# One tile or two for the small squares of a causal attention by elementwise products

## The chip, the cores and the metric

The kernel runs on one core of a Trainium2 chip. The metric is the device time of one execution in microseconds (us); lower is better. The engines are TensorE (PE in the profile), VectorE (DVE), ScalarE (ACT) and GpSimd (POOL); SyncE (SP) issues DMA transfers. Each engine works off its own queue in order, and semaphores tie the queues together.

## The reference

A block of four layers with residual additions on x of shape (8, 512, 256), all in float32: attention "a", a feed-forward network, attention "b" (ordinary causal attention, 16 heads of 16), and the same feed-forward network again. Attention "a" is the unusual one. It attends within each token's own features: per token and head, the 64 numbers of q, k and v are 64 positions of one feature, and the scores are the outer product of q and k under a causal mask.

```python
Q = (x @ Wq + bq).reshape(b, s, H, C) * inv_sqrt_c          # H = 16, C = 64
K = (x @ Wk + bk).reshape(b, s, H, C)
V = (x @ Wv + bv).reshape(b, s, H, C)
scores = jnp.einsum('bshq,bshk->bshqk', Q, K)                # an outer product per token and head
scores = jnp.where(jnp.triu(ones((C, C)), 1), -inf, scores)
attn = jnp.einsum('bshqk,bshk->bshq', softmax(scores), V).reshape(b, s, HID)
return attn @ Wo + bo
```

```python
h = silu(lin(x, w1) * w1_s) * (lin(x, w2) * w2_s)            # 256 -> 1024
h = gelu(lin(h, h1) * h1_s)                                  # 1024 -> 1024, twice
h = gelu(lin(h, h2) * h2_s)
return lin(h, w3) * w3_s                                     # 1024 -> 256
```

## The kernel before

Two streams run through the kernel at once. The first is attention "a" of batch b + 1, the second everything that follows for batch b (feed-forward, attention "b", feed-forward). The first uses POOL and DVE most, the second PE and ACT.

Attention "a" goes by units: one unit is 128 tokens (on the 128 partitions) and 4 of the 16 heads. There are 16 units a batch (4 groups of heads times 4 blocks of tokens) and 128 in all; "unit 9" below is the tenth of its batch. The causal triangle of 64 by 64 is cut into squares below the diagonal: one of 32 by 32, two of 16 by 16, four of 8, eight of 4, sixteen of 2, thirty-two of 1, and the diagonal. The squares of a unit are worked in four portions, `n_u`:

- 0 and 2: the squares of size 32, two heads each; 1: those of size 16; 3: all the small ones, sizes 8, 4, 2 and 1.
- Portions 0 to 2 have tiles `w` of 4096 columns, of which four rotate. Portion 3 has a tile `ws` of 2 x 1920 columns, and there is only one such tile.

The steps of a unit, each a method of `AttentionA`:

- `project` (PE, lines 841 and 846) and `keep_qk` (ACT): q, k and v of the unit.
- `scores` (line 893): the products of q and k. POOL makes those of portions 0, 1 and 2, in two halves of 1024 columns each; DVE makes the four of portion 3, one for each size (1024, 512, 256 and 128 columns), and the diagonal (line 872).
- `exps` (ACT, line 916; the diagonal at line 907): the exponentials, one instruction for each portion.
- `weigh` (DVE, lines 925 and 928): the exponentials times v, into the second half of the tile.
- `halve` (line 935): POOL issues a DMA that adds one half of the tile onto the other. `fold` (POOL, line 943) halves once more, for portion 2.
- `sums32` (PE, line 956, sixteen transposes, portion 0), `keep_sums`, `turn_sums` (line 1027) and `add32` (DVE, line 1038) sum portion 0 through PE. `gather` (DVE, line 1135) sums portions 1 and 2 and the sizes 8 and 4 of portion 3 by reductions.
- `adds` (POOL, line 1151) adds the rows that `gather` made to the unit's accumulator `acc`.
- `small_squares` (POOL): for size 2 it adds the two columns (line 1061, called the pair step below), and then adds the rows of size 2 and of size 1, straight from `ws`, to `acc` (line 1151 again). When these and `gather` are done, `ws` is free for the next unit.
- `invert` (DVE, line 1157), `divide` (POOL, line 1163), `turn_group` (PE), `keep_att` (ACT), `project_out` (PE), `new_x` (ACT): the quotient, the output projection and the new x.

The order on the engines is fixed by a table. Time is counted in slots, twelve to a unit; each row of `G['order']` gives a step its slot, counted from the unit's start, so that steps of up to four units lie side by side. Within a slot the row's place in the table decides. `G['first']` is the table of the first batch; from the second batch on, `G['shifts']` moves a step of one unit by some slots, and `G['bends']` moves the due time of the second stream in one unit. After each slot, the second stream is advanced by steps of an estimated length until it has caught up:

```python
            a.slot(at)
            ...
            due = at + 1 - 12 * NT * NG - 33
            due += BENDS[(at - 12) // 12 % (NT * NG)] if 0 < due < 12 * NT * NG * (NB - 1) else 0
            while spent * 12 * NT * NG < total * due:
                spent += next(done)
```

Of the second stream the text meets these: the row statistics of a new x (`moments`, DVE, line 600, after ACT's copy of the row at line 1472), the products of a hidden layer (PE, line 1453), and attention "b" with its scores (PE, lines 1599 and 1603), exponentials (ACT, line 1606) and values (PE, line 1611).

Of the kernel before, what the change touches and what calls it, by code (L numbers as in the profile page):

```python
# [16 lines left out]
P = 128  # L17
# [29 lines left out]
 'order': [[15, 'turn_sums', 0], [34, 'project_out'], [8, 'scores', 2, 1, 2], [10, 'exps', 2],  # L47
           [22, 'small_squares'], [-120, 'load'], [-26, 'normalise'], [6, 'exps', 1], [13, 'sums32', 0],
           [23, 'adds', 3], [16, 'keep16'], [9, 'weigh', 1], [-1, 'scores', 0, 0, 2], [20, 'add16'],
           [32, 'turn_group'], [-22, 'turn_x'], [11, 'fold', 0], [12, 'turn16'], [6, 'halve', 0],  # L50
           [11, 'scores', 3, 0, 1], [22, 'keep_sums', 2], [-30, 'ahead'], [14, 'sums16'], [22, 'add32', 2],
           [12, 'weigh', 2], [18, 'turn_sums', 2], [-8, 'project'], [10, 'halve', 1], [36, 'new_x'],
           [25, 'divide'], [13, 'weigh', 3], [7, 'scores', 2, 0, 2], [4, 'scores', 1, 1, 2], [17, 'fold', 2],
           [32, 'keep_att'], [-5, 'keep_qk'], [12, 'exps', 3], [12, 'halve', 2], [13, 'keep_sums', 0],
           [18, 'add32', 0], [18, 'gather', 3], [24, 'invert'], [13, 'gather', 1], [16, 'adds', 1],
           [20, 'sums32', 2], [4, 'weigh', 0], [3, 'exps', 0], [1, 'scores', 1, 0, 2], [-22, 'keep_x'],
           [0, 'scores', 0, 1, 2]],
# [3 lines left out]
           'order': [[21, 'small_squares'], [23, 'adds', 3], [21, 'sums32', 2], [-23, 'turn_x'],  # L61
                     [0, 'scores', 0, 1, 2], [4, 'scores', 1, 0, 2], [16, 'keep16'], [15, 'turn16'],
                     [29, 'divide'], [26, 'invert'], [19, 'add32', 0], [6, 'scores', 2, 0, 2],
                     [6, 'halve', 0], [-1, 'scores', 0, 0, 2], [-27, 'normalise'], [9, 'fold', 0],
                     [7, 'exps', 1], [10, 'exps', 2], [20, 'gather', 3], [15, 'turn_sums', 0],
                     [4, 'weigh', 0], [23, 'turn_sums', 2], [15, 'weigh', 3], [-120, 'load'], [-30, 'ahead'],
                     [17, 'adds', 1], [15, 'gather', 1], [19, 'sums16'], [10, 'scores', 3, 0, 1],
                     [23, 'add32', 2], [8, 'weigh', 1], [10, 'halve', 1], [36, 'new_x'],
                     [4, 'scores', 1, 1, 2], [13, 'weigh', 2], [-5, 'keep_qk'], [-20, 'keep_x'],
                     [6, 'scores', 2, 1, 2], [14, 'exps', 3], [31, 'turn_group'], [21, 'add16'],  # L70
                     [14, 'sums32', 0], [21, 'keep_sums', 2], [32, 'keep_att'], [13, 'fold', 2],
                     [14, 'keep_sums', 0], [-8, 'project'], [34, 'project_out'], [13, 'halve', 2],
# [16 lines left out]
 'shifts': [[6, 'gather', 1, 1], [5, 'project', 1], [7, 'add32', 2, 1], [13, 'weigh', 3, 1],  # L89
            [15, 'exps', 2, -1], [5, 'keep_sums', 2, -1], [15, 'scores', 2, 1, 2, 1], [4, 'project_out', -1],  # L90
            [13, 'adds', 3, -1], [5, 'divide', 1], [1, 'scores', 1, 1, 2, -1], [4, 'weigh', 0, 1],
            [14, 'scores', 0, 1, 2, 2], [8, 'gather', 3, 2], [11, 'weigh', 1, 1], [14, 'weigh', 2, -1],
            [7, 'scores', 1, 1, 2, -1], [2, 'normalise', 1], [2, 'turn_sums', 2, -1], [7, 'fold', 2, 1],
            [15, 'project', -1], [3, 'turn_sums', 0, 1], [12, 'turn_sums', 0, -1], [5, 'exps', 0, -1],
            [0, 'keep_att', 1], [9, 'turn_sums', 2, -1], [12, 'scores', 2, 0, 2, -2], [15, 'sums32', 0, -2],
            [1, 'turn_sums', 2, -1], [8, 'halve', 0, 1], [12, 'turn_sums', 2, -1], [15, 'add32', 0, -1],
            [11, 'turn_sums', 2, -1], [1, 'exps', 2, -1], [10, 'turn_sums', 2, 1], [4, 'scores', 0, 1, 2, -1],
            [5, 'gather', 3, 2], [5, 'exps', 1, -1], [10, 'scores', 2, 1, 2, 1], [13, 'gather', 1, -1],
            [13, 'gather', 3, -1], [4, 'divide', 1], [6, 'exps', 0, -2]],
 'bends': [0, 0, 0, 0, 0, 0, 0, 0.5, 0.5, 0, 0, 0, 1, 0, 0, -2],  # L100
 'sp': []}
# [244 lines left out]
def fast_path(ctx: ExitStack, tc: tile.TileContext, k, t, flag):  # L346
# [292 lines left out]
    units = (((32, 0, 2),), ((16, 0, 4),), ((32, 2, 2),), ((8, 0, 4), (4, 0, 4), (2, 0, 4), (1, 0, 4)))  # L639
    NU = len(units)  # L640
    SMALL = 1920
# [37 lines left out]
    def pieces(w, n, off, nsq, cols, b, n_u, parts):  # L679
# [7 lines left out]
        if n == 8 and kind8(b) == "pe":  # L687
            e, ev = (
                w[:, a * SMALL + off : a * SMALL + off + nsq * n * n].rearrange("p (j x i) -> p j x i", j=n, i=n)
# [3 lines left out]
        elif n < 16:  # L693
            e, ev = (
                w[:, a * SMALL + off : a * SMALL + off + nsq * n * n].rearrange("p (x i j) -> p x i j", i=n, j=n)
# [41 lines left out]
    BENDS = G.get("bends", [0] * NT * NG)  # L737

    class AttentionA:
# [126 lines left out]
        def scores(self, b, i, g, n_u, part, parts):  # L866
# [7 lines left out]
            if part == 0:  # L874
                if n_u < NU - 1 and (n_u != 1 or G["rot"] == 4):
                    w = wt.tile([P, 4096], F32, tag="w", name=f"w_{b}_{i}_{g}_{n_u}", bufs=G["rot"])
                elif n_u == 1:
                    w = wt.tile([P, 4096], F32, tag="w16", name=f"w16_{b}_{i}_{g}")
                else:
                    w = wt.tile([P, 2 * SMALL], F32, tag="ws", name=f"ws_{b}_{i}_{g}")  # L880
                self.live[b, i, g, n_u] = w
                self.ps = []
                for n, off, nsq, cols in squares(units[n_u]):
                    self.ps += list(pieces(w, n, off, nsq, cols, b, n_u, 2))
                if not hasattr(self, "pieces"): self.pieces = {}
                self.pieces[b, i, g, n_u] = self.ps
            ps = self.pieces[b, i, g, n_u]
            on_pool = n_u in (0, 2) or (n_u == 1 and part < p16(b)) or (n_u == 3 and "P3" in on(b))
            eng, q = (nc.gpsimd, kt[:, 1]) if on_pool else (nc.vector, qv[:, 0])
            mine = ps if parts == 1 else [ps[part]]  # L890
            for e, ev, rows, columns in mine:
                shape = list(e.shape)
                eng.tensor_tensor(  # L893
                    e, rows(q).to_broadcast(shape), columns(kt[:, 0]).to_broadcast(shape), ALU.mult
                )
# [7 lines left out]
        def exps(self, b, i, g, n_u):  # L903
# [8 lines left out]
            elif n_u < NU - 1:  # L912
                e = w.rearrange("p (b a r) -> p a b r", a=2, b=units[n_u][0][0] // JB)[:, 0]
            else:
                e = w[:, :SMALL]
# [14 lines left out]
        def halve(self, b, i, g, n_u):  # L930

            assert (b, i, g, n_u, "w") in self.seen
# [4 lines left out]
        def fold(self, b, i, g, n_u):  # L937

            if kind(b, n_u) == "pe16": return
# [5 lines left out]
        def sums32(self, b, i, g, n_u):  # L945

            how = kind(b, n_u)
            assert (b, i, g, n_u, "h" if how == "pe16" else "f") in self.seen
# [4 lines left out]
            n = 16 if how == "pe16" else 8  # L953
# [75 lines left out]
        def add32(self, b, i, g, n_u):  # L1029

            if kind(b, n_u) == "dve":
                self.adds(b, i, g, n_u)
                return
# [18 lines left out]
        def small_squares(self, b, i, g):  # L1052

            assert (b, i, g, NU - 1, "w") in self.seen
            self.seen.add((b, i, g, NU - 1, "s"))
            w = self.live[b, i, g, NU - 1]
            for n, off, nsq, cols in squares(units[NU - 1]):
                if n <= 2 and n not in reds(b):
                    both = self.columns_of(w, n, off, nsq)
                    if n == 2:  # L1060
                        (nc.vector if "small" in on(b) else nc.gpsimd).tensor_tensor(both[..., :1], both[..., :1], both[..., 1:], ALU.add)
                    self.add_rows(b, i, g, n, cols, both[..., 0], "small")
            self.done_small(b, i, g)

        def done_small(self, b, i, g):

            if all((b, i, g, NU - 1, what) in self.seen for what in ("r", "s") + (("8",) if kind8(b) == "pe" else ())):
                self.live.pop((b, i, g, NU - 1))

        def sums8(self, b, i, g):  # L1070

            if kind8(b) == "dve": return
            assert (b, i, g, NU - 1, "w") in self.seen
            self.seen.add((b, i, g, NU - 1, "8"))
            w = self.live[b, i, g, NU - 1]
            h = G.get("half8", 1)
            self.take(h, 0, 1)
            for r in range(2):
                for j in range(8):
                    nc.tensor.matmul(  # L1080
                        bank_half(h)[:, r * P : (r + 1) * P], w[:, r * SMALL + j * P : r * SMALL + (j + 1) * P], ident,
# [31 lines left out]
        def gather(self, b, i, g, n_u):  # L1113

            if n_u == 1 and kind(b, 1) != "dve": return
            assert (b, i, g, n_u, "h" if n_u < NU - 1 else "w") in self.seen
            self.seen.add((b, i, g, n_u, "r"))
            w = self.live[b, i, g, n_u]
            if n_u < NU - 1: self.live.pop((b, i, g, n_u))
# [20 lines left out]
        def adds(self, b, i, g, n_u):  # L1140
            if (b, i, g, n_u) not in self.sums: return
            for args in self.sums.pop((b, i, g, n_u)):
                self.add_rows(*args, f"adds{n_u}")
# [75 lines left out]

    class Weights:  # L1220
# [4 lines left out]
        def __init__(self):  # L1225
            def ffn():
                for i in range(MC // 4):
                    yield "gate", F32R, nc.gpsimd, t.w12p[i]
                for layer in range(2):
                    for i in range(MC // 2):  # L1230
                        yield "hidden", F32R, nc.gpsimd, t.h12[layer, i]
                yield "w3", F32R, nc.gpsimd, t.w3p

            def all_of_them():
                for b in range(NB):
                    yield from ffn()
                    yield "wbqk", F32, nc.sync, wbqk_d
                    yield "wbvp", F32, nc.sync, wbvp_d
                    yield from ffn()

            self.n, self.todo, self.loaded = 0, all_of_them(), []
# [3 lines left out]
        def ahead(self):  # L1245
            what = next(self.todo, None)
            if what is not None:
                name, dtype, eng, src = what
                w = hwp.tile([P, HB], dtype, tag="hw", name=f"{name}_{self.n}")[:, : src.shape[-1]]
                eng.dma_start(w, src)  # L1250
# [598 lines left out]
```

## Time and profile before

| | |
|---|---|
| median of 3 runs | 3597.4 us (3596.45 to 3601.86) |
| the profiled execution | 3604.64 us, of which the span in the profile is 3602.9 |
| busy in the span: DVE, PE, POOL, ACT | 3126.7, 3037.2, 2971.8, 2497.5 us |
| from 1245 to 1667 us (one batch of the steady part): DVE, POOL, PE, ACT | 389.1, 380.5, 363.5, 322.2 us of 422 |
| mean granted TensorE clock | 0.917 of full speed |

One execution was profiled. An entry such as "DVE ws L893" is an instruction of DVE from line 893 that writes tile `ws` (buffer numbers are left out). A list of waits gives, for a pair of engines and lines, the total idle time in us, how often it occurred and the longest one. In a row of a group the number behind `x` is the count, then come the busy time in us and the mean duration of one in ns, and behind the second bar the idle time in front of it with what ended it. In a timeline the columns are the start in us, the duration in us, the engine and the instruction; idle time of that engine just ahead of it stands in square brackets.

### The profile page before, as it was taken

Reading aid. Unit: us, or ns where it says so; the run is one execution under the profiler, and the core shown is the slowest. Engines: PE = TensorE matmul, PEld = TensorE weight load, DVE = VectorE, ACT = ScalarE, POOL = GpSimd, SP = SyncE. Lnnn points to the kernel's source line nnn. Section 1 sums busy time; section 2 is a strip of 40 time slices with the busy share of each in tenths; the row PEclk is TensorE's granted clock in tenths of the full one; section 3 lists DMA queues with packets and bytes.
Section 4 is the critical chain, followed back from the end, with each engine's and each line's share of the span. In section 5 each row is a group of like instructions: output and inputs, shape, how many; then the busy total and the mean of one; then the engine's idle time right before and its main releaser. Section 6 shows DMA issues by size and latency. Waiting matters only on the chain.

```text
span 3602.9 us, 42424 instructions
## 1 busy us (share of the span) xinstructions
PE 3037.2 (84%) x14468; PEld 2169.7 (60%) x14468; DVE 3126.7 (87%) x3844; ACT 2497.5 (69%) x3482; POOL 2971.8 (82%) x2682
## 2 busy tenths in 40 slices
PE   7765698798987998888986988879887889878998
PEld 4543475576746766466754766457664667556756
DVE  7999998999989998899988998899988999886226
ACT  4544587787867887688866877768766887665453
POOL 7999989988898989989898888989889898985010
PEclk8877699998998999999998989989999999989999
DMA  9877887698877988689976888779877888767414
GB/s 242 194 161 165 180 216 176 145 226 190 207 173 169 234 207 193 133 199 223 228 161 150 215 194 204 164 169 228 196 181 153 191 211 220 171 142 222 132 53 170
DMA packets 117038, 665.34 MB, mean 185 GB/s; under 512 B 12742, under 2 KB 30665, under 8 KB 43467
## 3 DMA queue, kind: packets, MB, share of 16 engines
q0 software_dynamic: 80640, 587.24, 71.2%
q1 hardware_dynamic: 35896, 75.02, 6.0%
q8 instruction: 116, 1.90, 0.2%
q14 instruction: 110, 0.90, 0.1%
q10 hardware_dynamic: 276, 0.27, 0.0%
HBM read 251.18 MB, written 8.65 MB: 72 GB/s over the span
## 4 chain that ended last, share of the span: by engine, by line
PE 31%; DVE 22%; POOL 21%; ACT 12%; issue 8%; DMA 5%; ACTq 0%; POOLq 0%; DVEq 0%
POOL w L893 10%; PE ph L1453 7%; DVE w L928 6%; DVE red L1135 5%; DMA w<-w 5%; POOL acc L1151 4%; PE pw L1381 4%; PE pyb L1611 4%; DVE ws L893 3%; PE bank L956 3%; PE pqkb L1532 3%; PE psb L1599 2%; POOL w L935 2%; ACT w L916 2%; DVE ws L928 2%
## 5 line engine op out<-in xcount | busy, mean ns | idle before, releaser
L893 POOL TENSOR_TENSOR w<-k 128x1024 f32<-128x1024 f32 x768 | 1617.4, 2195 | 31.2 <-PE bank L956 22.1
L1453 PE MATMUL ph<-h,hidden 128*128 128x512 f32 x4096 | 1012.1, 401 | 3.3 <-DVE h L1365 1.6
L928 DVE TENSOR_TENSOR w<-w,qv 128x1024 f32<-128x1024 f32 (+1 forms) x624 | 890.2, 1458 | 66.2 <-ACT w L916 66.0
L1453 PEld LDWEIGHTS ph<-h,hidden 128*128 128x128 f32 x4096 | 762.3, 189 | 181.1 <-issue 21.0
L916 ACT ACTIVATE w<-w 128x2048 f32<-128x2048 f32 x384 | 734.2, 1914 | 133.4 <-POOL w L893 131.1
L935 POOL DMA_DIRECT2D w<-w x384 | 353.1, 919 | 167.6 <-DVE w L928 63.6
L1381 PE MATMUL pw<-xnt,gate 128*128 128x512 f32 (+2 forms) x1152 | 347.1, 455 | 147.3 <-ACT silu L1356 85.5
L1135 DVE TENSOR_REDUCE red<-w 128x256 f32<-128x2048 f32 x240 | 426.7, 1778 | 25.5 <-DMA w<-w 24.1
L1135 DVE TENSOR_REDUCE red<-ws 128x256 f32<-128x2048 f32 (+1 forms) x256 | 435.6, 1742 | 0.0
L1151 POOL TENSOR_TENSOR acc<-acc,red 128x256 f32<-128x256 f32 x496 | 389.6, 785 | 31.4 <-DVE red L1135 12.6
L893 DVE TENSOR_TENSOR ws<-qv,k 128x1024 f32<-128x1024 f32 (+3 forms) x512 | 300.1, 647 | 98.9 <-POOL acc L1151 98.7
L1381 PEld LDWEIGHTS pw<-xnt,gate 128*128 128x128 f32 x1152 | 238.9, 226 | 229.6 <-ACT silu L1356 103.1
L956 PE MATMUL bank<-ident,w 128*128 128x128 f32 x2304 | 329.4, 305 | 44.2 <-ACT x L1202 19.7
L956 PEld LDWEIGHTS bank<-ident,w 128*128 128x128 f32 x2304 | 305.0, 160 | 72.5 <-ACT x L1202 31.7
L943 POOL TENSOR_TENSOR w<-w 128x1024 f32<-128x1024 f32 x112 | 279.4, 2495 | 63.1 <-DMA w<-w 63.0
L928 DVE TENSOR_TENSOR ws<-ws,qv 128x1024 f32<-128x1024 f32 (+3 forms) x512 | 294.9, 637 | 15.1 <-ACT ws L916 14.7
L916 ACT ACTIVATE ws<-ws 128x1920 f32<-128x1920 f32 x128 | 233.3, 1822 | 84.3 <-DVE ws L893 80.4
L846 PE MATMUL qv<-wqv,xnta 128*128 128x512 f32 x512 | 263.8, 641 | 27.2 <-DVE ws L928 24.9
L1419 DVE TENSOR_TENSOR h<-ph,h 128x512 fp32r<-128x512 f32 x256 | 169.6, 684 | 109.4 <-ACT ph L1415 103.2
L1606 ACT ACTIVATE eb<-psb 128x512 f32<-128x512 f32 (+3 forms) x503 | 182.0, 461 | 88.1 <-PE psb L1603 87.8
L1414 ACT ACTIVATE h<-ph,s_sb 128x512 fp32r<-128x512 f32 x256 | 176.6, 690 | 88.2 <-PE ph L1453 86.4
L1157 DVE RECIPROCAL acc<-acc 128x256 f32<-128x256 f32 x128 | 223.2, 1744 | 4.0 <-POOL acc L1151 3.4
(163 smaller groups left out, 4851.5 us busy)
## 6 DMA issues: line engine op xcount, KB each, us to landing
w<-w POOLq DMA_DIRECT2D x384, 1024.0 KB, 7.7
hidden<-in_h POOLq DMA_DIRECT2D x128, 1024.0 KB, 6.6
gate<-in_w12p POOLq DMA_DIRECT2D x32, 1024.0 KB, 6.4
w<-in_w3p POOLq DMA_DIRECT2D x16, 1024.0 KB, 8.8
wqv<-wqv_d SPq DMA_DIRECT2D x31, 512.0 KB, 4.0
wo<-in_wo SPq DMA_DIRECT2D x32, 256.0 KB, 3.9
w<-in_h SPq DMA_DIRECT2D x8, 1024.0 KB, 6.7
wk<-wk_d SPq DMA_DIRECT2D x31, 256.0 KB, 5.3
```

What stands on the lines that cost most here:

```text
L846: nc.tensor.matmul(qv.rearrange("p j f -> p (j f)"), xnt[:, c, :], wqv[:, c, :], start=(c == 0), stop=(c == DC - 1),)
L893: eng.tensor_tensor(e, rows(q).to_broadcast(shape), columns(kt[:, 0]).to_broadcast(shape), ALU.mult)
L916: nc.scalar.activation(e, e, AF.Exp, scale=C**-0.5)
L928: nc.vector.tensor_tensor(ev, e, columns(qv[:, 1]).to_broadcast(list(e.shape)), ALU.mult)
L935: nc.gpsimd.dma_start(w[:, :2048], w[:, 2048:], accum_op=ALU.add)
L943: nc.gpsimd.tensor_tensor(w[:, :1024], w[:, :1024], w[:, 1024:2048], ALU.add)
L956: nc.tensor.matmul(bank_half(G["half"][4])[:, :P], w[:, j * P : (j + 1) * P], ident, start=(j == 0), stop=(j == n - 1), is_transpose=True,)
L1135: nc.vector.tensor_reduce(red, self.columns_of(w, n, off, nsq), AX.X, ALU.add)
L1151: (nc.vector if what == "psum" or what in on(b) else nc.gpsimd).tensor_tensor(rows, rows, part.rearrange("p a (x i) -> p a x i", i=n), ALU ...
L1157: nc.vector.reciprocal(acc[:, 0, :], acc[:, 0, :])
L1381: nc.tensor.matmul(pj[:, toks], w[:, m % 4, j, c, :], xs[:, p, c, toks], start=(p == 0 and c == 0), stop=(p == 1 and c == DC - 1),)
L1453: nc.tensor.matmul(pss[j], w[:, j, c, :], h_in(p, c), start=(p == 0 and c == 0), stop=(p == 1 and c == MC - 1),)
```

## The change

Portion 3 is cut in two. Portion 3 now holds sizes 8 and 4 in a tile of 2 x 1536 columns, and a new portion 4 holds sizes 2 and 1 in a tile of 2 x 384 columns; together they take the space of the old tile. There is one tile of each. `scores`, `exps` and `weigh` are called once for each, so ACT has two exponentials where it had one. The tile of portion 3 is free when `gather` has read it; the tile of portion 4 when POOL's row steps have.

`small_squares` becomes `pair`, `rows 2` and `rows 1`, and `adds 3` becomes `adds 3 8` and `adds 3 4`: each is a row of the table by itself. The instructions in them are the same as before. The tables and shifts are new, and one bend is (unit 9, from 0 to −0.5). Some rows of the diff change no instruction: `'on': ['adds0']` and `kinds` name an addition that this kernel makes in another way, portion 0's `fold`, portion 2's `turn_sums` and `keep_sums`, and the steps `turn16`, `keep16`, `sums16` and `add16` return at once here, `sp` is empty, and `pe32` is used by no table.

```diff
- 'order': [..., [22, 'small_squares'], ..., [23, 'adds', 3], ..., [25, 'divide'], ..., [11, 'scores', 3, 0, 1],
-           [13, 'weigh', 3], [12, 'exps', 3], [18, 'gather', 3], [1, 'scores', 1, 0, 2], ...]
+ 'order': [..., [22, 'pair'], [22, 'rows', 2], [22, 'rows', 1], ..., [23, 'adds', 3, 8], [23, 'adds', 3, 4],
+           [1, 'scores', 1, 0, 2], ..., [11, 'scores', 3, 0, 1], [11, 'scores', 4, 0, 1], [13, 'weigh', 3], [13, 'weigh', 4],
+           [12, 'exps', 3], [12, 'exps', 4], [18, 'gather', 3], ..., [25, 'divide'], ...]
...
- 'bends': [0, 0, 0, 0, 0, 0, 0, 0.5, 0.5, 0, 0, 0, 1, 0, 0, -2],
+ 'bends': [0, 0, 0, 0, 0, 0, 0, 0.5, 0.5, -0.5, 0, 0, 1, 0, 0, -2],
...
-    units = (((32, 0, 2),), ((16, 0, 4),), ((32, 2, 2),), ((8, 0, 4), (4, 0, 4), (2, 0, 4), (1, 0, 4)))
+    units = (((32, 0, 2),), ((16, 0, 4),), ((32, 2, 2),), ((8, 0, 4), (4, 0, 4)), ((2, 0, 4), (1, 0, 4)))
     NU = len(units)
-    SMALL = 1920
+    LARGE, SMALL = 3, {3: 1536, 4: 384}
...
                 else:
-                    w = wt.tile([P, 2 * SMALL], F32, tag="ws", name=f"ws_{b}_{i}_{g}")
+                    w = wt.tile([P, 2 * SMALL[n_u]], F32, tag=f"ws{n_u}", name=f"ws{n_u}_{b}_{i}_{g}")
...
-            elif n_u < NU - 1:
+            elif n_u < LARGE:
                 e = w.rearrange("p (b a r) -> p a b r", a=2, b=units[n_u][0][0] // JB)[:, 0]
             else:
-                e = w[:, :SMALL]
+                e = w[:, : SMALL[n_u]]
             nc.scalar.activation(e, e, AF.Exp, scale=C**-0.5)
...
-        def small_squares(self, b, i, g):
+        def pair(self, b, i, g):
...
+                if n == 2:
+                    both = self.columns_of(w, n, off, nsq)
+                    (nc.vector if "small" in on(b) else nc.gpsimd).tensor_tensor(both[..., :1], both[..., :1], both[..., 1:], ALU.add)
+
+        def rows(self, b, i, g, size):
...
+                if n == size:
+                    self.add_rows(b, i, g, n, cols, self.columns_of(w, n, off, nsq)[..., 0], "small")
...
-        def adds(self, b, i, g, n_u):
-            if (b, i, g, n_u) not in self.sums: return
-            for args in self.sums.pop((b, i, g, n_u)):
-                self.add_rows(*args, f"adds{n_u}")
+        def adds(self, b, i, g, n_u, n):
+            for args in self.sums.get((b, i, g, n_u), []):
+                if args[3] == n:
+                    self.add_rows(*args, f"adds{n_u}")
```

The lists of instructions of both kernels, engine by engine, hold the same instructions but for ACT's (128 exponentials of 1920 columns become 128 of 1536 and 128 of 384). Waits that stand by themselves go from 896 to 1000 on POOL, from 919 to 797 on DVE and from 1497 to 1553 on ACT; table loads stay at 377. Within a batch from the second on, these stand in another order:

| engine | in another place than before |
|---|---|
| POOL | in nearly every unit the first half of the size 16 products ahead of the division, which stood ahead of both halves; unit 3's second half of portion 0 ahead of unit 2's last halving, and unit 4's behind unit 3's, where it was the other way round; the row addition of size 16 of unit 4 behind unit 5's fold and halving of portion 0; the addition of portion 2's rows of units 6 and 14 behind unit 7's and 15's halving of portion 1; of unit 7, the first half of unit 9's portion 0 ahead of the small row additions; unit 13's fold ahead of its row addition of size 16 |
| DVE | unit 3's weighing of portion 1 ahead of unit 2's reduction of portion 2; the four row statistics of the second stream's new x ahead of unit 8's weighing of portion 0 and its diagonal; unit 12's weighing of sizes 2 and 1 behind its reduction of size 16; one feed-forward product ahead of unit 13's weighing of portion 1; unit 14's diagonal behind unit 13's small products; unit 13's `add32` ahead of its reductions |
| ACT | copies of units 3, 9, 10 and 11 and unit 10's exponential of portion 1 by two to eight places among the second stream's |
| PE | unit 9's sixteen transposes of portion 0 ahead of a group of attention "b" products; unit 2's projection, the turn of units 0 and 12, and the output projection of units 9 and 13 by up to four matrix products of a hidden layer or of attention "b" |

## The prediction

> **What bounds the kernel now.** I read the windows first: a batch's sixteen units repeat every 422 us from 400 to 3300 us, the attention alone fills the front, and the last 253 us have no attention of the first kind in them.
>
> ```profile
> core 0: us, PE busy (x) PEld busy (x) DVE busy (x) ACT busy (x) POOL busy (x), PEclk, DMA share, GB/s
> ...
> 1245.00:1667.00 422.00, 363.48 (x1762) 260.54 (x1760) 389.10 (x491) 322.22 (x446) 380.49 (x347) 0.94 0.82 192
> ...
> 3350.00:3603.00 253.00, 235.16 (x1204) 174.40 (x1202) 105.19 (x148) 108.30 (x215) 17.09 (x36) 0.96 0.34 116
> ```
>
> In a batch DVE is busy 389 of 422 us and POOL 380; PE has 363, ACT 322. DVE and POOL take turns as the bound, and each idles mostly for the other. Then the list of waits:
>
> ```profile
> ACT w L916 <- POOL w L893: 131.1, 76, 5.0
> ...
> DVE ws L893 <- POOL acc L1151: 98.7, 72, 3.4
> ...
> ACT ws L916 <- DVE ws L893: 80.4, 44, 3.4
> ...
> DVE w L928 <- ACT w L916: 66.0, 60, 4.4
> ...
> POOL w L943 <- DMA w<-w: 63.0, 36, 5.5
> ...
> POOL w L935 <- ACT ws L916: 50.7, 31, 3.8
> ```
>
> (total us, times, longest). The second line is the one the change is at. There is one `ws` tile, so DVE may not write the next unit's products until POOL has added the last row of the size 1 squares out of it. The timeline, DVE, ACT and POOL alone, shows one such wait and its length, 2.99 us in brackets:
>
> ```profile
> 2249.57 0.42 DVE L872 TENSOR_TENSOR acc<-qv,k 128x256 f32<-128x256 f32 x1
> 2250.31 0.88 POOL L1061 TENSOR_TENSOR ws<-ws 128x256 f32<-128x256 f32 x1
> ...
> 2251.27 1.67 POOL L1151 TENSOR_TENSOR acc<-acc,ws 128x256 f32<-128x256 f32 x2
> ...
> 2252.97 2.35 DVE L893 TENSOR_TENSOR ws<-qv,k 128x1024 f32<-128x1024 f32 x4 [2.99 <-POOL acc L1151]
> ```
>
> DVE stands idle until POOL's pair step and both row steps are through, and behind the four products in DVE's queue is the weighing (L928) that POOL's next halving (L935) needs. Prices come from the groups kept apart by form:
>
> ```profile
> L916 ACT ACTIVATE ws<-ws 128x1920 f32<-128x1920 f32 x128 | 233.3, 1822 | 84.3 <-DVE ws L893 80.4 <-POOL acc L1151 3.6
> L907 ACT ACTIVATE acc<-acc 128x256 f32<-128x256 f32 x128 | 54.7, 427 | 0.5
> L893 DVE TENSOR_TENSOR ws<-qv,k 128x1024 f32<-128x1024 f32 x128 | 156.1, 1219 | 98.9 <-POOL acc L1151 98.7
> L893 DVE TENSOR_TENSOR ws<-qv,k 128x512 f32<-128x512 f32 x128 | 86.9, 679 | 0.0
> ```
>
> **Part 1, two tiles.** The tile of sizes 8 and 4 is free once DVE's own reductions (L1135) are through, so its two products, 1219 + 679 ns = 1.90 us, no longer wait for POOL; the 413 and 279 ns of sizes 2 and 1 still do. Each wait shrinks by up to 1.90 us. Read one by one in the trace, the waits lose 80 of their 98.7 us. That is the most it can bring; the least is nothing, where POOL sets the pace anyway. On the path: following the chain that ended last step by step, it goes from POOL's adding straight to DVE's `ws` product 18 times; those waits sum to 24 us, of which 22 go. Off the chain, 11 of POOL's 31 waits at the halving, 12 us, come within 8 us of such a DVE wait; I count half of it. Term: −28 (0 to −80). Late next in these places is the weighing's wait for ACT (66.0 us) and what is left for the small tile.
>
> **Part 2, ACT.** 128 exponentials become 256. Between 256 and 1920 columns the two rows give (1822 − 427)/1664 = 0.838 ns a column, so 1536 columns take 1500 ns and 384 take 534: +0.21 us a unit, +27 us in all. No table load is added, since the two stand side by side. ACT has 100 us idle in 422, and this covers it; uncovered it costs the 27. `ws` exponentials hold 33 of the chain's us (400 to 3300), 14% of the 233, hence +4; the first is 0.32 us shorter, which shortens the 10 waits of the weighing for it (14.7 us) by 3. Term: +1 (−3 to +27).
>
> **Part 3, POOL beside a busier DVE.** POOL's score products (L893) take 1.94 us at the shortest and 2.24 in the median, 13% apart; the five that ran with DVE idle took 1.96 on average, the 646 wholly covered by DVE work 2.20. If that is contention, filling 80 us of DVE's idle time slows POOL by 10 us, none if not. Term: +3 (0 to +10). The Trainium skill, "SBUF — State Buffer", section "Who interferes with whom", says that a DVE instruction with at most one SBUF input outside the two-port modes does not contend with GpSimd. The products here read one input from PSUM and one from SBUF, so by that rule this term would be 0 and the sum 3 us lower.
>
> **Part 4, single steps.** POOL's pair, rows and adds keep number, size and, in the main table, their adjacent places: 0. The semaphore instructions go up by 104 on POOL and down by 122 on DVE, at 17 and 21 ns: under 3 us either way.
>
> **Part 5, order.** The first half of the size 16 products goes ahead of the division in nearly every unit. POOL's wait for the reciprocal there totals 3 us and may go; the division comes 2.2 us later, but its reader, PE's turn, stands seven slots (about 15 us) on. If that cover were gone, 2.2 us a unit. Term: −2 (−3 to 0).
> The other moves, with seven batches behind the first:
> - Unit 3: a weighing (2.34 us) ahead of a 1.21 us reduction, so a halving can leave 1.2 us earlier: at most −8; I take −4.
> - Units 4, 6 and 14: a row addition (0.88, 0.46, 0.46 us) goes behind a halving, whose transfer starts that much earlier; POOL's folds wait 63 us for transfers. At most −13, taken −6. Units 3 and 4 exchange a 2.2 us product with a halving in opposite senses: 0.
> - Unit 8: the four row statistics, 4 × 0.9 us with their small steps, go ahead of weighing 0 (2.7 us). ACT's copies of the four new rows (L1472) have a gap of 2.4 to 4.9 us before the third or fourth in each of the seven batches, and in the last two DVE already waits 4.0 and 2.6 us in it. So this puts a wait in DVE's queue where there was work, and POOL's halving 0 and PE's transposes are behind it. 0 to +35, taken +5, nearer to the covered side because DVE reaches that point when two or three rows are ready in five batches, and their 0.9 us each run while the next come.
> - Unit 9: sixteen transposes go ahead of a group of second-attention matmuls. They stood 2.7 to 5.5 us behind the landing of their tile, about what they are moved by: 0 to +14, taken 0.
> Unnamed moves on PE and ACT change places with one to four neighbours: ±10, taken 0. Together −5 (−31 to +59).
>
> **Sum.** −28 + 1 + 3 − 2 − 5 = −31. The profiled execution took 3604.64 us (span 3602.9 and 1.7 around it), so 3573.6; the median of the runs is 7.2 us lower, which gives 3566.
>
> **Rivals.**
> *DVE's time comes back in full* (0.13): the 80 us, and ACT's earlier start hides its 27. For it: DVE is the busiest engine. Against: only 18 of 72 waits are on the chain. 3597.4 − 80 + 4 = 3521.
> *POOL is the bound where DVE waits* (0.10): averaged over six batches, units 9 and 11 hold 3.0 and 2.4 us of this DVE wait, and there POOL idles only 0.5 and 1.0 us; DVE would then only wait later, for POOL's next product. Against: the chain does cross this edge. Part 1 shrinks to −8 and the moves to 0, which gives 3591, and 3599 without those 8; I take 3594.
> *Slower: the statistics ahead of weighing 0* (0.15). Place: unit 8 of each batch; DVE stops for ACT's rows, POOL's halving 0 is late, then the transposes. Price 35 us, with 10 from POOL's slowing, 8 from ACT, and Part 1 cut to −14: +39, 3636. It decides from (31 + 5)/7 = 5.1 us a batch on the path.
>
> **How the numbers follow.** The forecast, part of Part 1 on the path and the order near neutral, has 0.62 and alone would range from 3545 to 3590. The range reaches to the full gain below and to the nearer part of the slower case above, 3520 to 3612. A measurement here tells 0.2%, 7.2 us, from no change: faster is below 3590.2, the forecast and the first rival, 0.75; same 0.10; slower 0.15.
>
> **What would show it.** In the profile after: the wait of DVE's `ws` product for POOL's adding under 35 us where 98.7 was; two `ws` exponentials near 1500 and 534 ns; ACT busy about 27 us more; a batch near 418 us; POOL's L893 mean up by less than 30 ns. Wrong would be: that wait gone and the batch still 422 us (POOL bound), a DVE wait of over 4 us a batch at the statistics (L600), or DVE's wait for ACT at the weighing grown by as much as the other shrank.

## The result

| | before | after |
|---|---|---|
| median of 5 runs each, same chip | 3598.21 us (3596.45 to 3601.86) | 3572.35 us (3568.92 to 3580.34) |
| ratio | 1 | 0.9929, 95% interval 0.9914 to 0.9943 |
| profiled execution, its span | 3604.64, 3602.9 us | 3572.35, 3570.6 us |
| granted clock, mean | 0.917 | 0.922 |

The change makes the kernel 25.5 us faster by the ratio (0.0071 of 3598 us), where −31 us was forecast. The profile after has other line numbers, since the diff moved the code: the products of q and k are L919 (L893 before), the exponentials L942 (L916), the weighing L954 (L928), the halving L962 (L935), the fold L970 (L943), the reductions L1170 (L1135), the additions L1186 (L1151) and the reciprocal L1192 (L1157). The groups of the profile after, kept apart by form (count, then busy us and mean ns, then the idle time in front):

```profile
L919 POOL TENSOR_TENSOR w<-k 128x1024 f32<-128x1024 f32 x768 | 1611.2, 2186 | 26.8 <-PE bank L983 13.9 <-DVE red L1170 8.3 <-DVE ws L954 2.9
L942 ACT ACTIVATE ws<-ws 128x1536 f32<-128x1536 f32 x128 | 192.3, 1503 | 33.2 <-DVE ws L919 32.9
L919 DVE TENSOR_TENSOR ws<-qv,k 128x1024 f32<-128x1024 f32 x128 | 155.3, 1213 | 0.0
L942 ACT ACTIVATE ws<-ws 128x384 f32<-128x384 f32 x128 | 66.9, 523 | 0.3
L919 DVE TENSOR_TENSOR ws<-qv,k 128x256 f32<-128x256 f32 x128 | 53.0, 414 | 14.9 <-POOL acc L1186 14.6
```

The first product of the small squares no longer waits at all (0.0 in the third row, where 98.9 was); what is left of the wait, 14.6 us, stands at the small tile's first product. The two exponentials take 1503 and 523 ns. POOL's score products are not slower: 2186 ns on average, and 2195 in the profile before:

```profile
L893 POOL TENSOR_TENSOR w<-k 128x1024 f32<-128x1024 f32 x768 | 1617.4, 2195 | 31.2 <-PE bank L956 22.1 <-DVE red L1135 7.5 <-ACT k L863 1.2
```

So far it reads as the forecast. The list of DVE's waits in the profile after (total us, times, longest) shows the other side:

```profile
DVE h L1464 <- ACT ph L1460: 96.0, 70, 7.1
DVE w L954 <- ACT w L942: 84.4, 69, 4.4
...
DVE red L1170 <- DMA w<-w: 42.6, 26, 6.6
DVE acc L1192 <- POOL acc L1186: 30.5, 24, 2.6
...
DVE ws L919 <- POOL acc L1186: 14.6, 18, 2.5
DVE st L620 <- ACT x L1517: 10.1, 6, 7.2
...
DVE ws L954 <- ACT ws L942: 6.3, 8, 2.0
```

Of the same list before, the prediction shows the waits of 98.7 and 66.0 us. Three more are:

```profile
DVE red L1135 <- DMA w<-w: 24.1, 20, 5.7
...
DVE st L600 <- ACT x L1472: 14.0, 4, 7.2
...
DVE acc L1157 <- POOL acc L1151: 3.4, 2, 2.7
```

The wait at the `ws` product fell by 84.1 us, from 98.7 to 14.6. But the weighing's wait for ACT rose from 66.0 to 84.4, the reduction's wait for a halving from 24.1 to 42.6, and the reciprocal's wait for POOL's additions from 3.4 to 30.5. These three take back 18.4 + 18.5 + 27.1 = 64.0 us. DVE waits less at one place and, by three quarters of that, more at three others. The timeline of the profile after, at unit 9 of the batch in which the prediction showed a wait of 2.99 us (start, duration, idle time in brackets), shows how:

```profile
2222.25 0.88 POOL L1087 TENSOR_TENSOR ws<-ws 128x256 f32<-128x256 f32 x1
...
2223.21 1.67 POOL L1186 TENSOR_TENSOR acc<-acc,ws 128x256 f32<-128x256 f32 x2
2223.26 0.41 DVE L894 TENSOR_TENSOR acc<-qv,k 128x256 f32<-128x256 f32 x1
2223.59 2.34 DVE L919 TENSOR_TENSOR ws<-qv,k 128x1024 f32<-128x1024 f32 x4
...
2227.35 2.36 POOL L1186 TENSOR_TENSOR acc<-acc,red 128x128 f32<-128x128 f32 x3
...
2229.44 1.93 ACT L942 ACTIVATE ws<-ws 128x1536 f32<-128x1536 f32 x2
...
2229.74 1.75 DVE L1192 RECIPROCAL acc<-acc 128x256 f32<-128x256 f32 x1 [1.55 <-POOL acc L1186]
...
2231.41 2.28 DVE L954 TENSOR_TENSOR ws<-ws,qv 128x1024 f32<-128x1024 f32 x4
```

DVE starts its four small products while POOL is still at its row steps, without a wait, and then stands 1.55 us at the reciprocal, for the three additions that POOL makes a little later. Whether the 25 us come from the tiles at all is therefore open after this profile, and the experiments take the change apart.

### The profile page after: what moved, and what is told of

It is laid out like the page before. It is cut to its first block, busy times and chain, and to the rows that moved or that the text cites. A ratio compares the mean times of both kernels' runs of the same rounds, so it can differ in the third digit from the quotient of the medians.

```text
span 3570.6 us, 42600 instructions
## 1 busy us (share of the span) xinstructions
PE 3031.4 (85%) x14468; PEld 2166.1 (61%) x14468; DVE 3121.9 (87%) x3844; ACT 2508.7 (70%) x3610; POOL 2965.4 (83%) x2682
## 4 chain that ended last, share of the span: by engine, by line
PE 32%; DVE 21%; POOL 19%; ACT 10%; issue 9%; DMA 9%; POOLq 0%; ACTq 0%; DVEq 0%
POOL w L919 9%; DMA w<-w 8%; PE ph L1498 6%; DVE w L954 6%; DVE red L1170 6%; POOL acc L1186 4%; PE pw L1426 4%; PE bank L983 4%; PE pyb L1656 4%; PE pqkb L1577 3%; PE psb L1644 2%; ACT w L942 2%; POOL w L962 2%; PE qv L868 2%; DVE ws L954 2%
## 5 line engine op out<-in xcount | busy, mean ns | idle before, releaser
L919 POOL TENSOR_TENSOR w<-k 128x1024 f32<-128x1024 f32 x768 | 1611.2, 2186 | 26.8 <-PE bank L983 13.9
L954 DVE TENSOR_TENSOR w<-w,qv 128x1024 f32<-128x1024 f32 (+1 forms) x624 | 890.5, 1458 | 85.0 <-ACT w L942 84.4
L942 ACT ACTIVATE w<-w 128x2048 f32<-128x2048 f32 x384 | 734.4, 1915 | 132.3 <-POOL w L919 130.8
L1170 DVE TENSOR_REDUCE red<-w 128x256 f32<-128x2048 f32 x240 | 427.1, 1780 | 46.7 <-DMA w<-w 42.6
L962 POOL DMA_DIRECT2D w<-w x384 | 347.8, 906 | 136.5 <-DVE w L954 65.6
L1426 PE MATMUL pw<-xnt,gate 128*128 128x512 f32 (+2 forms) x1152 | 334.6, 442 | 138.8 <-ACT silu L1401 92.5
L1170 DVE TENSOR_REDUCE red<-ws 128x256 f32<-128x2048 f32 (+1 forms) x256 | 435.7, 1742 | 0.0
L1186 POOL TENSOR_TENSOR acc<-acc,red 128x256 f32<-128x256 f32 x496 | 389.8, 786 | 41.2 <-DVE red L1170 23.4
L1426 PEld LDWEIGHTS pw<-xnt,gate 128*128 128x128 f32 x1152 | 229.0, 218 | 220.8 <-ACT silu L1401 112.3
L983 PEld LDWEIGHTS bank<-ident,w 128*128 128x128 f32 x2304 | 306.5, 161 | 90.7 <-ACT x L1237 42.8
L970 POOL TENSOR_TENSOR w<-w 128x1024 f32<-128x1024 f32 x112 | 275.8, 2462 | 81.8 <-DMA w<-w 81.1
L919 DVE TENSOR_TENSOR ws<-qv,k 128x1024 f32<-128x1024 f32 (+3 forms) x512 | 301.4, 646 | 14.9 <-POOL acc L1186 14.6
L954 DVE TENSOR_TENSOR ws<-ws,qv 128x1024 f32<-128x1024 f32 (+3 forms) x512 | 295.2, 637 | 6.3 <-ACT ws L942 6.3
L942 ACT ACTIVATE ws<-ws 128x1536 f32<-128x1536 f32 (+1 forms) x256 | 245.1, 1013 | 33.4 <-DVE ws L919 32.9
L1192 DVE RECIPROCAL acc<-acc 128x256 f32<-128x256 f32 x128 | 223.5, 1746 | 31.3 <-POOL acc L1186 30.5
```

Source lines behind the costliest of these rows:

```text
L919: eng.tensor_tensor(e, rows(q).to_broadcast(shape), columns(kt[:, 0]).to_broadcast(shape), ALU.mult)
L942: nc.scalar.activation(e, e, AF.Exp, scale=C**-0.5)
L954: nc.vector.tensor_tensor(ev, e, columns(qv[:, 1]).to_broadcast(list(e.shape)), ALU.mult)
L962: nc.gpsimd.dma_start(w[:, :2048], w[:, 2048:], accum_op=ALU.add)
L970: nc.gpsimd.tensor_tensor(w[:, :1024], w[:, :1024], w[:, 1024:2048], ALU.add)
L983: nc.tensor.matmul(bank_half(G["half"][4])[:, :P], w[:, j * P : (j + 1) * P], ident, start=(j == 0), stop=(j == n - 1), is_transpose=True,)
```

## The experiments

Each kernel had five rounds against the kernel before on the same chip, though not all on one chip; the medians of the kernel before lie between 3596 and 3603 us in them. A ratio is to the kernel before; to set two of the kernels side by side I subtract their ratios, turn them into us with 3598, and add the half widths of the intervals in quadrature. That gives ±7 to 8 us against the kernel after, so differences of 3 or 4 us say only that nothing large is there.

**The two halves of the change.** First the tiles alone: the code of after with the order, the shifts and the bends of before.

```diff
+    units = (((32, 0, 2),), ((16, 0, 4),), ((32, 2, 2),), ((8, 0, 4), (4, 0, 4)), ((2, 0, 4), (1, 0, 4)))
 in the order of before:
- [22, 'small_squares']         + [22, 'pair'], [22, 'rows', 2], [22, 'rows', 1]
- [23, 'adds', 3]               + [23, 'adds', 3, 8], [23, 'adds', 3, 4]
- [11, 'scores', 3, 0, 1]       + [11, 'scores', 3, 0, 1], [11, 'scores', 4, 0, 1]
- [13, 'weigh', 3]              + [13, 'weigh', 3], [13, 'weigh', 4]
- [12, 'exps', 3]               + [12, 'exps', 3], [12, 'exps', 4]
```

> The two tiles with the order, shifts and bends of the kernel before: portion 4 stands directly behind portion 3 in each table. The forecast's sum for the split alone (parts 1 to 3) is -24 us, 3574 where before has 3598, and DVE's wait of the ws product for POOL's adding falls from 99 to under 35 us. If POOL is the bound where DVE waits, the wait falls as far, but the time stays at 3590 to 3598. If the gain of the whole change is in the new order, 3595 to 3600.

Measured: 3596.34 us, before 3603.32, ratio 0.9989 (0.9976 to 1.0001): −4 us, not told from no change. DVE's waits in its profile:

```profile
DVE w L933 <- ACT w L921: 91.8, 70, 4.4
...
DVE red L1149 <- DMA w<-w: 42.2, 36, 6.1
...
DVE ws L898 <- POOL acc L1165: 20.4, 21, 2.5
DVE acc L1171 <- POOL acc L1165: 16.3, 9, 2.6
```

The wait for POOL (L898) fell by 78 us, as the tiles are meant to do, and hardly any time came of it: the weighing (L933), the reduction (L1149) and the reciprocal (L1171) wait 57 us more than in the profile before. The one profiled execution took 3586.78 us, the shortest of its twelve, so the profile is not that of a slower kernel. It is a pair of single executions that the two profiles compare, 18 us apart, and net of these four places DVE waits 21 us less; what the tiles are worth is told by the ratio over all rounds.

Then the order alone: one tile and one exponential, in the order, shifts and bends of after.

```diff
 in the order of after:
- [22, 'pair'], [22, 'rows', 2], [22, 'rows', 1]     + [22, 'small_squares']
- [23, 'adds', 3, 8], [23, 'adds', 3, 4]             + [23, 'adds', 3]
- [11, 'scores', 4, 0, 1], [12, 'exps', 4], [13, 'weigh', 4], and the shifts of portion 4
```

> One tile for the small squares with the order, shifts and bends of the kernel after (the steps of portion 4 fall together with those of portion 3, the row steps with the pair step). The forecast's sum for the order alone (part 5) is -7 us: 3591, with ends of 3564 and 3657. If the gain of the whole change is in the new order, 3572 to 3580. If the order is only good for two tiles, 3605 or more.

Measured: 3581.26 us, ratio 0.9941 (0.9925 to 0.9957): −21 us, and its profile still has the whole wait:

```profile
DVE ws L901 <- POOL acc L1159: 94.2, 77, 3.4
DVE w L936 <- ACT w L924: 58.4, 55, 4.4
```

So the gain of 21 us came with 94.2 us of the wait still in place, and taking the wait away without the order brought some 4 us, at most 9. The two halves, −4 and −21, add up to the −25.5 of both.

**ACT's second exponential, by itself.** The kernel before with one tile, but the exponential cut in two:

```diff
-            nc.scalar.activation(e, e, AF.Exp, scale=C**-0.5)
+            if n_u == NU - 1:
+                for part in (slice(0, 1536), slice(1536, SMALL)):
+                    nc.scalar.activation(e[:, part], e[:, part], AF.Exp, scale=C**-0.5)
```

> The kernel before with its small squares' exponential cut into two instructions of 1536 and 384 columns; one tile, order as before. The forecast's price of the second instruction on the path is +4 us (3602), with DVE's wait of the ws product unchanged near 99 us. If ACT had no cover it would be +27 us, 3625. If the shorter first exponential were what helps, below 3595; it should not, since DVE's weighing of the sizes reads one tile.

Measured: 3598.38 us, before 3603.32, ratio 0.9989 (0.9974 to 1.0004). The instructions take 1502 and 521 ns, and the added 0.2 us a unit are not seen in the time: uncovered they would be 27 us, and the interval ends at +1.4. So the tiles' gain is not eaten by the price of the second exponential. That ACT's idle time is what covers it fits the profile and was not tried by itself.

**The rest of the wait.** In the order of after, DVE's products for sizes 2 and 1 go one slot later, behind a weighing:

```diff
- [11, 'scores', 4, 0, 1] (behind [11, 'scores', 3, 0, 1])
+ [12, 'scores', 4, 0, 1] (behind [12, 'weigh', 2])
```

> The kernel after, with the products of sizes 2 and 1 behind the weighing of portion 2 on DVE (slot 12 in place of 11, from the second batch on). The 14.6 us of DVE's wait for POOL's adding that are left should go to under 4. If such waits are still on the path, the time falls by a quarter of it, 3 to 5 us, to 3568; if DVE only meets the next wait (for ACT's exponentials, for the transfers), nothing changes within 0.2%; if ACT's later second exponential delays the weighing of the small squares, 3575 to 3585.

Measured: 3579.38 us, ratio 0.9930 (0.9912 to 0.9947), the same as after. The 14.6 us of the `ws` wait are gone from the list, and the weighing waits for ACT 110.0 us where it waited 84.4. Again a DVE wait went and another grew, and the time stayed.

**Where in the order the gain is.** The kernel after with the shifts and bends of before (the tables of after stay):

> The kernel after with the shifts and bends of the kernel before; the two tables and the two tiles as after. By the forecast's part 5 the moves of single units are worth 5 us: 3577. If these moves hold the order's gain, 3588 to 3596. If the tables hold it, 3570 to 3578.

Measured: 3592.53 us, ratio 0.9978 (0.9967 to 0.9990), 18 ± 7 us above after. Most of the gain goes with the rows that move single steps of single units. The division's swap, the tables' clearest move, was tried alone, with `[25, 'divide']` ahead of `[1, 'scores', 1, 0, 2]` again:

> The kernel after with the division back ahead of both halves of the size 16 products (main table; all else as after). By the forecast's part 5 this swap is worth 2 us: 3574 where after has 3572. If this swap, the one move that recurs in nearly every unit, holds the order's gain that the one-tile run showed (about 20 us), 3585 to 3595.

Measured: 3578.47 us, ratio 0.9938 (0.9924 to 0.9952): 3 us above after, within the spread.

Of the shifts, units 8 to 10 went back to those of before. Of the rows dropped, `[8, 'weigh', 0, 1]` puts the four row statistics behind unit 8's weighing 0 again and `[10, 'exps', 1, -1]` puts unit 10's exponential of portion 1 later on ACT; the others move no more than a copy on ACT and an output projection on PE, once a batch.

```diff
- [8, 'weigh', 0, 1], [8, 'scores', 2, 1, 2, 1], [9, 'project_out', 1], [9, 'gather', 3, 2], [10, 'exps', 1, -1],
- [10, 'keep_att', 1], [10, 'turn_sums', 2, -1], [10, 'keep_sums', 2, -1], [9, 'fold', 0, 1], [10, 'fold', 0, -1]
+ [10, 'turn_sums', 2, 1]
```

> The kernel after with the shifts of units 8, 9 and 10 of the kernel before: the row statistics stand behind unit 8's weighing of portion 0 again, and ACT's exponential of unit 10's portion 1 behind four of attention b's. The forecast priced the statistics' move at +5 us (0 to +35), so undoing it should bring 3567. If the move is a gain, because it lets the second stream's normalisation start earlier, unit 9 is 1.6 us longer here, as with all old shifts, and the time is 7 x 1.6 = 11 us higher, 3583. If the order's gain is spread thinly, 3570 to 3576.

Measured: 3583.72 us, before 3596.37, ratio 0.9958 (0.9944 to 0.9971): 10 ± 7 us above after. So this group of moves brings time rather than costing it. DVE's timeline in one batch, first of the profile after, then of this kernel:

```profile
1790.47 0.42 DVE L620 BATCH_NORM_STATS2 st<-x 128x6 f32<-128x256 f32 x1
...
1794.00 2.28 DVE L954 TENSOR_TENSOR w<-w,qv 128x2048 f32<-128x2048 f32 x1
```

```profile
1797.61 2.28 DVE L947 TENSOR_TENSOR w<-w,qv 128x2048 f32<-128x2048 f32 x1
1799.81 0.42 DVE L613 BATCH_NORM_STATS2 st<-x 128x6 f32<-128x256 f32 x1
```

No idle time stands in brackets at the statistics in either. Counted from DVE's diagonal product of unit 7, the last statistics of batches 1 to 6 end at 39.9, 39.9, 40.7, 40.9, 43.5 and 50.5 us after, and at 42.4, 42.8, 42.8, 43.6, 44.6 and 51.0 us here; attention "b"'s first projection on PE starts 0.3 to 2.4 us later here, 7.7 us in the sum of the six. So the second stream starts earlier with the statistics ahead, and the weighing's delay did not cost as much. The rival is unit 10's exponential, which this run moves too. In these two profiles, by DVE's diagonal products (L894 after, L887 here), a batch is 2.5 us longer here on average over six, 1.6 of it between those of units 9 and 10, and in all six batches the exponential, the copy and the output projection all come behind unit 10's; 0.7 us are between those of units 10 and 11, where the exponential can have a part. This is how I read the traces; no run moves the statistics and nothing else.

Units 2 to 4 with the shifts of before:

> The kernel after with the shifts of units 2, 3 and 4 of the kernel before; all else as after. In the profiles unit 4 is 1.2 us shorter in after than with the old shifts, and POOL's wait for a w tile that PE still reads falls from 38 to 14 us. If the gain of the order is local to units 4 and 9, this costs 7 x 1.2 = 8 us: 3580. If it is spread thinly over all the moves, under 4 us: 3572 to 3576.

Measured: 3580.39 us, ratio 0.9938 (0.9925 to 0.9951): 3 ± 7 us above after, which settles nothing on these units. The bend of unit 9 was taken back in the kernel after, and put by itself into the kernel before:

> The kernel after with the bend of unit 9 back at 0: sixteen transposes of portion 0 and ACT's copies of sums, q and k stand behind some of attention b's work again. The forecast took this move as worth 0, with a cost of up to 14 us. In the profiles unit 9 is 1.6 us shorter in after than with the old shifts and bends. If the bend makes that, 7 x 1.6 = 11 us: 3583. If it is worth nothing, 3572; if it costs what the forecast feared, below 3570.

> The kernel before with the bend of unit 9 at -0.5 as its only change: one tile, old tables, old shifts. If the bend by itself is a gain, 11 us: 3588 where before has 3599, and unit 9 1.2 us shorter or more. If it is only good beside the other moves, no change. If PE now stops for the transfer, slower by up to 14 us.

Measured: 3570.73 us, ratio 0.9917 (0.9903 to 0.9932), and 3601.15 us, ratio 0.9999 (0.9990 to 1.0008). Without the bend the kernel after is 4 ± 7 us faster, and with it the kernel before is unchanged to 3 us: no gain of the bend is seen.

**The reciprocal's new wait.** Is the 30.5 us wait of the reciprocal worth removing? In the kernel after, the reciprocal goes behind the next unit's weighing of sizes 2 and 1, and the division to the end of slot 28:

```diff
- [24, 'invert'], [25, 'divide']
+ [25, 'invert'] (behind [13, 'weigh', 4]), [28, 'divide'] (last)
```

> The kernel after with DVE's reciprocal behind the weighing of the small squares and POOL's division behind the second half of the size 16 products, from the second batch on. The wait of the reciprocal for POOL's adding, 30.5 us in after and 3.4 in before, should fall under 5 us. If a DVE wait for POOL is worth a quarter of itself, 3565. If POOL is the bound wherever DVE waits for it, as the run of the split alone suggests, the idle time turns up in other waits of DVE and the time stays within 0.2% of 3572. If the division is now late for the accumulator's reader, 3580 or more.

Measured: 3601.24 us, ratio 0.9998 (0.9986 to 1.0009): all of the gain is lost, 25 ± 7 us. DVE's waits in its profile:

```profile
DVE red L1166 <- DMA w<-w: 72.9, 47, 6.4
DVE ws L950 <- ACT ws L938: 53.1, 25, 3.9
```

and, from the list of all engines, those of PE's turn (L1204) for the division (L1194), then the only one of this kind in the profile after:

```profile
PEld bank L1204 <- POOL acc L1194: 36.4, 15, 7.2
...
PE bank L1204 <- POOL acc L1194: 23.9, 14, 6.8
```

```profile
PEld bank L1208 <- POOL acc L1198: 6.0, 1, 6.0
```

The reciprocal's wait is down to 0.4 us, but DVE now waits 53.1 us for ACT's exponential of the small squares (6.3 us in the profile after) and 72.9 us for halvings (42.6), and POOL's additions wait for DVE's reductions 41.1 us (23.4). In the timeline of the profile after (unit 9, above) the reciprocal, 1.75 us, had been the work beside which ACT's exponentials ran, and the weighing of the small squares (L954) started right behind both. But the run moves two steps. The division now comes late for its reader, a price that the expectation names: PE's turn waits for it in 15 places where it waited in one. Which of the two makes the 25 us, no run here tells.

**A wait of POOL itself.** In the profile after POOL's fold waits 81.1 us for its transfer, in that before 63.0. One fold a batch, unit 5's, goes two slots later, behind the next unit's first halving and POOL's first half of portion 2; only POOL's order changes.

```diff
+ [5, 'fold', 2, 2]
```

> The kernel after with the fold of unit 5 two slots later, behind the next unit's first halving and first half of portion 2's products. POOL waits 4.6 us a batch there for the transfer that the fold reads. If that wait is on the path, it saves up to 7 x 4 = 28 us: 3545. If, as with the earlier waits, the next engine is the bound there, nothing: 3568 to 3576. If DVE's reduction of the folded tile becomes late, 3576 to 3585.

Measured: 3563.75 us, ratio 0.9896 (0.9881 to 0.9910), 12 ± 7 us below after. POOL's waits in its profile:

```profile
POOL w L958 <- DVE w L950: 61.6, 44, 3.8
POOL w L966 <- DMA w<-w: 44.7, 32, 3.7
...
POOL w L958 <- DVE acc L1061: 29.0, 9, 4.1
```

The fold's wait (L966) is 36.4 us shorter; 29.0 us return at a halving (L958), where the profile puts them down to DVE's sum of portion 0. The program is the fastest of all that were run, 37 us below the kernel before.

## Why the prediction was right or wrong

The time and the sign were right (−25.5 us, −31 forecast), and most of the signs that it named came: the `ws` wait under 35 us (14.6), exponentials near 1500 and 534 ns (1503 and 523), POOL's products no slower. ACT's busy time grew by 11 us and not by 27. The batches, counted on DVE's diagonal product from unit 0 to unit 0, went from 419.3 to 414.4 us on average, where 418 was forecast for a batch of 422: the same −4 to −5. But the right sum came out of wrong terms: the tiles were priced far too high and the order far too low, and that the two errors nearly cancel is luck.

- *Part 1, two tiles, −28.* This is the step that failed: a term mis-sized, with −4 us measured for Parts 1 to 4 together (ratio 0.9989, 0.9976 to 1.0001). The wait went as counted, 78 of 98.7 us. What failed is the count by the chain that ended last. It passed through 18 of these waits, and I took each as time that would go. With the tiles alone the chain passes through none of them, and in the run of the order alone, 21 us faster, still through 16. DVE, set free, stood at the next thing that was late: ACT's exponential, a halving, POOL's additions. That at each such place another branch had ended nearly as late is my reading of these waits, not shown place by place. The prediction named the first of them as late next and gave it no price. The rival that DVE "would then only wait later, for POOL's next product", with 0.10 and Part 1 at −8, was near in size, but only 13 of the 57 us came back as a wait for POOL, and not for a product. What the prediction took as evidence against it, that the chain crosses this edge, did not hold. Of the signs named for a wrong forecast, DVE's wait for ACT at the weighing grew, but by 18 us and not by as much as the other shrank.
- *Part 2, ACT, +1.* Right: the second instruction by itself did not show in the time (−4, from −9 to +1). ACT's busy time went from 2497.5 to 2508.7 us only, since other groups got 15 us shorter in sum; the exponentials themselves went from 233.3 to 259.2, +26 where +27 was worked out.
- *Part 3, POOL beside a busier DVE, +3.* 0: the mean went from 2195 to 2186 ns with DVE busier beside it (2579.8 us between 400 and 3200, 2555.6 before). The durations of about 1.94 and 2.24 us that made me allow for it are no sign of a slower POOL: the longer records overlap the next instruction's. For 522 of the products in the profile before, the next POOL instruction starts before the product's record ends, and it starts 1.92 us after the product did, on average, whether the product is recorded with under 2.05 us (117 of them) or with more; the same holds where DVE is busy throughout (375, 1.92 us) and where it is busy for less than 0.3 of the time (13, 1.91 us). This agrees with the Trainium skill, "SBUF — State Buffer", section "Who interferes with whom", by which a DVE instruction with at most one SBUF input, outside the two-port modes, does not contend with GpSimd.
- *Part 4, single steps, 0.* Not tried by itself; it lies in the −4 us of the tiles.
- *Part 5, order, −5, with −2 for the division.* Measured −21 (ratio 0.9941, 0.9925 to 0.9957) for both, inside the ends −34 to +59 and far from the value taken. One of its terms looks to have the wrong sign: the statistics ahead of unit 8's weighing, taken +5 (0 to +35), are in a group of rows worth 10 ± 7 us of gain. I priced what would wait behind them and not who waits for them: PE's attention "b", which begins with these rows. The wait at the statistics that I feared went from 14.0 to 10.1 us. The division's swap and units 2 to 4 (3 us each) and the bend are not told from zero. Some 18 us are in the shifts as a whole; what is not in units 8 to 10 lies in others, and stays open.
- *The rivals.* DVE's time in full is excluded by the tiles alone. The slower case is excluded by the time, and the group of moves with its mechanism is a gain.

## What to carry to other kernels

Idle time of one engine that waits for another as busy as itself was not a price here, and neither was its place on the chain that ended last: take the wait away alone, with all else as it was, before it is put in a sum, and look for its time at the next place where the freed engine meets a late partner (78 us of wait, 4 us of time). Small moves in the order can be worth more: one fold moved by two slots brought 12 us, and a group of moves that put four short statistics in front of a weighing about 10. These are single tries, not a rule. When a change brings a structure together with a new order, run each without the other; here the order was nearly the whole of it.

## What the runs showed that I had not expected

Taking a wait away can cost time. The reciprocal's 30.5 us of waiting went when it and the division were moved, and the kernel became 25 ± 7 us slower, with 53.1 us of DVE's waits for ACT where 6.3 had been, and 15 waits of PE for the division where one had been. And a recorded duration need not be the time for which an engine is held: POOL's products of 1.96 and of 2.24 us both let the next instruction start after 1.92.
